# A gated cross-attention layer and a mixture of eight experts on one core: when the first rows, weights and output rows are moved, and which engine copies what

## The chip, the core and the metric

The kernel runs on one core of a Trainium2 chip. The core's engines take their instructions in program order, each from a queue of its own: TensorE (PE, with its weight loads shown apart as PEld), VectorE (DVE), ScalarE (ACT), GpSimd (POOL) and SyncE (SP). SP and POOL also start transfers (DMA); sixteen DMA engines move the bytes. The metric is the device time of one execution in microseconds (us). For the kernel before, three executions gave 212.71, 212.73 and 213.91 us, so a median of 212.73 us.

## The reference, cut to what matters

The input `x` is 4 batches of 256 rows of 256 numbers, `ctx` 4 x 256 x 128. First an attention layer adds to `x`, then a layer of experts adds to the sum:

```
query = ctx @ Wq.T + bq ;  key = ctx @ Wk.T + bk
attention = softmax(query @ key.T)
x = x + tanh(g0) * (layernorm(x) @ attention.T)          # per batch

xf = layernorm(x)
probs = softmax(gelu(xf @ rw1) @ rw2)
wgt, idx = top_k(probs, 2)                               # two of eight experts for each row
for e in range(8):
    Ye = gelu(xf @ w1[e] + b1[e]) @ w2[e] + b2[e]        # w1: 256 x 1024, w2: 1024 x 256
    Ce = gelu(b1[e]) @ w2[e] + b2[e]                     # what the expert gives for a row of zeros
    for k in range(2):
        mask = idx[:, k] == e ;  active = any(mask)
        out += active * wgt[:, k] * where(mask, Ye, Ce)
x = x + tanh(g1) * out
```

A row that did not choose expert e still receives `Ce`, weighted, if anybody chose it. So the output is x, plus for each row a constant part (a sum over experts of `Ce`), plus for its two chosen experts the difference `Ye - Ce`.

## The kernel before, in words

**Attention and router.** The 1024 rows are eight tiles of 128. Batches 0 to 2 (six tiles, "early") go through attention and the router first, in an order written by hand in a string (`order`, L446 to L453); batch 3 follows as steps that are woven into later work. Steps have names: `po` the attention product, `add` the sum into `acc` (the running x in SBUF), `sf`, `pf`, `xf` the second layer norm and its write to the table `rows` in DRAM (L367), `ow` the write of `acc` to the output in DRAM (L356). A step's name and a key (`ow:3`: batch 3; 2a and 2b are the two tiles of batch 2) make an entry.

**Slots.** The choices are sorted by expert into slots of 128 rows; a slot has one expert. Slots 0 to 4 hold early rows (NA = 5), slots 5 and up the rest; with this input 19 slots are used. Slots 0 to 15 are written out statically, 16 and up stand in conditional blocks. For each slot:
- `gather` (L764, on POOL) brings its 128 rows from `rows` by an index list (`take`), an indirect DMA;
- `fill` (L135, on SP) brings the expert's `w1` (1 MB); SP first reads the expert's number from the tile `who` (L893, `expert`). Slot 0's comes in two halves;
- `turn` transposes the rows on PE (L779) and copies them out of PSUM into `xs` (L781);
- `first_layer`: 8 chunks of four matmuls (L796), each closed by a gelu on ACT (L800); after four chunks DVE subtracts gelu(b1) (L803);
- `second_layer`, one slot behind: sixteen matmuls (L815) with `w2`, which lies in SBUF for all experts (`w2:5`, `w2:3` load it, L126); DVE scales the result by the rows' weights (L818) and POOL adds it into the output by an indirect DMA with add (L820).

Four PSUM banks take the first layer's results, two the second layer's, two (`bank_x`) the transposes and small products.

**Constants.** For every expert, DVE forms `gelu(b1) @ w2` down to 128 partial sums (`bias_path`, L842, eight instructions an expert, on the row `b2` loaded by `b2_`, L833 and L834) and adds it into `both` (L849, L851). One product with ones on PE (`sums1`, L875) adds the partitions, `sums2` (L878) copies it out of PSUM, `constant_row` (L884, L886) makes each tile's constant from it, and `add_constants` (L889, POOL) adds all to the output in one 1 MB DMA with add.

**Weaving.** Batch 3's router, the lists of the later slots, biases and constants are entries of two lists, `main` and `second`. `first_layer` and `second_layer` call `between` after every chunk, so sixteen times a slot; a call adds to a credit (0.45 us, less where DVE has work of the slot itself, at most 1.0 in all) and takes entries whose cost the credit still covers. A number in a list is a pause of so many calls. Entries issued in a call stand behind that chunk in every engine's queue:

```
credit = min(credit + us, 1.0)
...
if isinstance(queue[0], tuple) and queue[0][0] > 0 and credit < (-1.0 if name == "main" else 0.0):
    break
```

Where work between attention and slot 0 stands is written out (the block that begins with `do("cnt:0 tra:3 ...")`): index lists of the early slots, batch 3's attention, `gather:0`, `gather:1`, `fill:0` and `fill:1`, `turn(0)`.

Of the kernel before, what the change touches and what calls it, by code (L numbers as in the profile page):

```python
# [10 lines left out]
I32 = mybir.dt.int32  # L11
AF = mybir.ActivationFunctionType
# [7 lines left out]
def gated_xattn_moe_kernel(  # L20
# [417 lines left out]
    def w2_(n):  # L438
# [10 lines left out]
        attT:0 st:3 pw:3 xn:3 exp:1 po:0 attT:2 norm:1 po:2a add:0 pt:1 sf:0 po:2b attT:1 add:2a po:1 pf:0 add:2b sf:2a xf:0  # L449
        pf:2a add:1 trf:0 sf:2b xT:0 sf:1 pf:2b r:0 gel:0 xf:2b pf:1 xf:2a trf:2b lg:0 xT:2b trf:2a xf:1 w2:3  # L450
        r:2b xT:2a chosen:0 trf:1 gel:2b r:2a xT:1 lg:2b gel:2a chosen:2b r:1 lg:2a qk:3 gel:1 gb1 table:Exp q:3 k:3
        chosen:2a lg:1 chosen:1 ow:0 ow:2a ow:2b ow:1
    """  # L453
    MANUAL = {
        mybir.EngineType.PE, mybir.EngineType.Activation, mybir.EngineType.DVE, mybir.EngineType.Pool,
# [3 lines left out]
    def do(text):  # L459
        for step in text.split():  # L460
            kind, _, key = step.partition(":")
            steps[kind](key)
# [63 lines left out]
    nc.gpsimd.memset(runs1[:, 0:1], 0.0)  # L526
    nc.gpsimd.memset(runs2[:, 0:1], 0.0)

    hqs1 = last.tile([P, GA, P], BF16, name="hqs1")

    class Go:
# [240 lines left out]
    def turn(s, xs):  # L772

        if s >= NS:
            return
        xg = xgs.pop(s)
        ps = bank_x(f"xt_{s}")
        for c in range(DC):
            nc.tensor.transpose(ps[:, ts(c, P)], xg[:, ts(c, P)], ident)  # L779
        copy = nc.scalar.copy if s < NA else nc.vector.tensor_copy  # L780
        copy(xs, ps[:, 0:D].rearrange("p (c l) -> p c l", c=DC))  # L781
        xss[s] = xs

    def nothing(_):
# [24 lines left out]
    def second_layer(s, hT, between=nothing):  # L809
        go, j = of(s)  # L810
        e = nc.tensor.value_load(go.who[0:1, j : j + 1], min_val=0, max_val=E - 1)
        w2_sb = w2_all[:, bass.ds(e, 1)][:, 0]
        ps = bank_y(f"y_{s}")
        for i in range(IC):
            nc.tensor.matmul(ps[:, 0:D], lhsT=hT[:, i, :], rhs=w2_sb[:, i, :], start=(i == 0), stop=(i == IC - 1))  # L815
            between(0.45 - ((0.4 if s < NA else 0.8) if i == IC - 1 else 0.0))
        ys = slotp.tile([P, D], F32, tag="ys", bufs=4, name=f"ys_{s}")
        nc.vector.tensor_scalar(ys, ps[:, 0:D], go.share[:, j : j + 1], None, ALU.mult)  # L818
        last_row = EARLY * P if s < NA else T
        nc.gpsimd.indirect_dma_start(  # L820
            out=total[0:last_row, :], out_offset=bass.IndirectOffsetOnAxis(ap=go.give[:, j : j + 1], axis=0),
            in_=ys, in_offset=None, compute_op=ALU.add, bounds_check=last_row - 1, oob_is_err=False,
        )
# [56 lines left out]
    def constant_row(t, k):  # L880

        at = k * EARLY + t if t < EARLY else GA + k * LT + t - EARLY
        if k == 0:
            nc.vector.tensor_scalar(acc[:, t, :], sums[:, 0, :], wgt[:, at, :], None, ALU.mult)  # L884
        else:
            nc.vector.scalar_tensor_tensor(acc[:, t, :], sums[:, 1, :], wgt[:, at, :], acc[:, t, :], ALU.mult, ALU.add)  # L886

# [2 lines left out]

    def expert(s):
        go, j = of(s)
        return nc.sync.value_load(go.who[0:1, j : j + 1], min_val=0, max_val=E - 1)  # L893

    filled = 0

# [29 lines left out]
            inv_(i, g)  # L926

    with tc.manual_schedule(engines=MANUAL):
        do("cnt:0 tra:3 pc:0 scan en:3 xnT:3 over:0 runs:0 nmax:3 lead:0 exp:3 rank:0 pos:0 split:0 rden:3 put:0 norm:3 pt:3 attT:3")
        hqs_inv(0)  # L930
        do("past:0 who:0 fill:0 lists:0 gather:0 sel:0 soft:0 po:3 gather:1 fill:1")
        for i in range(2):
            bias_(0, i, 0, 1)
        do("wgt:0 add:3 table:Gelu ow:3")
        turn(0, transposed_rows(0))
        do("sf:3 pf:3 gather:4")
        for v in range(3):
            piece_(0, v)


        def each_(f, *args):
            return [(0.0, lambda a=a: f(*a)) for a in args]

        def w(cost, text):
            return cost, lambda: do(text)

        def f(cost, fn, *a):
            return cost, lambda: fn(*a)

        main = [  # L950
            3, w(.65, "xf:3"), 3, w(0, "trf:3"), 1, w(0, "xT:3"), 3, w(0, "r:3"), w(0, "gel:3"), 3, w(0, "lg:3"), 1,
            w(1.4, "chosen:3"), w(.2, "cnt:1"), 4, w(0, "pc:1"), w(.35, "scan"), w(.3, "soft:1"), w(.7, "over:1"),
            w(.3, "runs:1"), w(.5, "past:1"), w(.5, "who:1"), w(.45, "lead:1"), w(.4, "rank:1"), w(1.3, "pos:1"),
            w(.75, "split:1"), w(.6, "put:1"),
        ]
        for g in range(0, G, 4):
            main += [f(.16, hq_, 1, h) for h in range(g, g + 4)]
            main += [2] if g == 0 else []
            main += [f(0, inv_, 1, h) for h in range(g - 4, g)] if g else []
        main += [1] + [f(0, inv_, 1, h) for h in range(G - 4, G)] + [  # L960
            1, w(.35, "lists:1"), w(0, "gather:8 fill:7"), "lists", w(.25, "sel:1"),
        ]
        third = XS // 3
        main += [f(1.3, bias_, 1, i, 0, third) for i in range(2)] + ["biases 5", w(1.0, "wgt:1")]
        main += [f(.8, piece_, 1, v) for v in range(3)] + [2] + [f(0, inw_, 1, g) for g in range(G)] + [
            1, w(.25, "share:1"), "shares 1"] + [
            f(1.3, bias_, 1, i, lo, lo + third) for lo in (third, 2 * third) for i in range(2)] + ["biases 11"]
        main += [f(.2, act1_, 0), f(.2, act1_, 1), 2, f(0, act2_, 0), 1, f(.2, act3_, 0)]
        for e in range(E):
            main += [f(0, b2_, e)] if e else [f(0, b2_, 0)]  # L970
            main += [f(.47, bias_path, e, c) for c in range(IC)] + [f(.47, both_, e, k) for k in range(K)]
        main += [2, f(0, sums1_, 0), 2, f(.8, sums2_, 0)]
        main += [f(.47, constant_row, t, k) for t in range(NT) for k in range(K)] + [f(0, add_constants, 0)]
        second = [f(.6, bias_, 0, i, 1, 2) for i in range(2)] + ["biases 1"]
        second += [f(1.2, bias_, 0, i, 2, NA) for i in range(2)] + ["biases 2"]
        second = [5] + [f(0, inw_, 0, g) for g in range(GA)] + [2, w(.25, "share:0"), "shares 0"] + second
        queues = {"main": main, "second": second}
        credit, pause = 0.0, {"main": 0, "second": 0}
        reached = set()

        def one_item(name, forced=False):

            nonlocal credit
            item = queues[name].pop(0)
            if isinstance(item, str):
                reached.add(item)
            elif not isinstance(item, int):
                credit -= item[0]
                item[1]()
            elif not forced:  # L990
                pause[name] = item

        def between(us):
            nonlocal credit
            credit = min(credit + us, 1.0)
            for name, queue in queues.items():
                pause[name] = max(pause[name] - 1, 0)
                while queue and not pause[name]:
                    if isinstance(queue[0], tuple) and queue[0][0] > 0 and credit < (-1.0 if name == "main" else 0.0):
                        break  # L1000
                    one_item(name)

        def by_now(name, mark):
            while mark not in reached:
                one_item(name, forced=True)

        pending = None
        for s in range(FIX):
            if s > NA:
                gather_to(s + AHEAD)  # L1010
            if 0 < s < NA - 2:
                fill_to(s + 2)
            elif s > NA:
                fill_to(min(s + 2, FIX + 1))
            if s == NA - 1:
                by_now("main", "lists")
            if s > 0:
                turn(s + 1, transposed_rows(s + 1))
            if s in (1, 2):
                by_now("second", f"biases {s}")  # L1020
            if s in (NA, NA + third):
                by_now("main", f"biases {s}")
            hT = hidden(f"hT_{s}")
            first_layer(s, hT, between)
            if pending is not None:
                if pending[0] == 0:
                    by_now("second", "shares 0")
                if pending[0] == NA:
                    by_now("main", "shares 1")
                second_layer(*pending, between)  # L1030
            pending = (s, hT)
            if s == 0:
                turn(1, transposed_rows(1))
        assert gathered > FIX + AHEAD - 1 and filled == FIX + 2, (gathered, filled)
        while main:
            one_item("main", forced=True)
# [70 lines left out]
```

## Time and profile before

| | |
|---|---|
| median of three executions | 212.73 us |
| the profiled execution's own time | 212.38 us |
| its span, first to last instruction | 210.6 us |
| PE busy | 178.9 us, 85% |
| DVE busy | 142.2 us, 68% |
| ACT busy | 80.1 us, 38% |
| POOL busy | 72.7 us, 34% |
| moved by DMA | 38.76 MB, mean 184 GB/s |
| mean granted TensorE clock | 0.954 |

The profile is that of one execution. Its times count from the first instruction, so 1.8 us of the execution's time lie around the span. "Busy" is the time in which an engine executes; how long it waited, and what ended the wait, stands beside the groups of instructions. The clock is what the chip granted TensorE: 1.00 is full speed.

### The profile page before, as it was taken

Reading aid. Unit: us, or ns where it says so; the run is one execution under the profiler, and the core shown is the slowest. Engines: PE = TensorE matmul, PEld = TensorE weight load, DVE = VectorE, ACT = ScalarE, POOL = GpSimd, SP = SyncE. Lnnn points to the kernel's source line nnn. Section 1 sums busy time; section 2 is a strip of 40 time slices with the busy share of each in tenths; the row PEclk is TensorE's granted clock in tenths of the full one; section 3 lists DMA queues with packets and bytes.
Section 4 is the critical chain, followed back from the end, with each engine's and each line's share of the span. In section 5 each row is a group of like instructions: output and inputs, shape, how many; then the busy total and the mean of one; then the engine's idle time right before and its main releaser. Section 6 shows DMA issues by size and latency. Waiting matters only on the chain.

```text
span 210.6 us, 3835 instructions
## 1 busy us (share of the span) xinstructions
PE 178.9 (85%) x1198; PEld 159.7 (76%) x1198; DVE 142.2 (68%) x424; ACT 80.1 (38%) x210; POOL 72.7 (34%) x89
## 2 busy tenths in 40 slices
PE   2999762829799997999999999997499999999940
PEld 1866561619699897999999999995299989999830
DVE  1999888842478969978299999999589332242200
ACT  2582664404545143254245225423032451353100
POOL 5408200451008066041604422504531612545241
PEclk9999999676999999999999999999789999999995
DMA  6899999794793982225376678599502285332321
GB/s 180 243 329 351 335 293 341 244 335 177 251 344 70 366 299 76 28 25 199 78 291 181 192 226 251 209 373 372 160 7 48 47 111 91 50 54 31 55 30 20
DMA packets 23688, 38.76 MB, mean 184 GB/s; under 512 B 2440, under 2 KB 17808, under 8 KB 23664
## 3 DMA queue, kind: packets, MB, share of 16 engines
q1 hardware_dynamic: 18208, 32.16, 44.5%
q0 software_dynamic: 4880, 6.17, 16.8%
q8 instruction: 13, 0.21, 0.4%
q10 hardware_dynamic: 576, 0.13, 0.3%
q14 instruction: 11, 0.09, 0.1%
HBM read 33.21 MB, written 5.64 MB: 184 GB/s over the span
## 4 chain that ended last, share of the span: by engine, by line
DVE 20%; PE 14%; issue 12%; DMA 10%; POOL 2%; POOLq 0%; ACT 0%; DVEq 0%
DVE gsum L842 12%; PE h L796 7%; DMA out<-ys,give 6%; PE y L815 6%; DVE hT L803 4%; DMA out<-ys,take 3%; DVE both L851 2%; DVE ys L818 1%; PE cst L875 1%; POOL xg L764 1%; DVE xs L781 1%; POOL out L820 1%; DMA b_row<-in_b 1%; PE xt L779 0%; ACT hT L800 0%
## 5 line engine op out<-in xcount | busy, mean ns | idle before, releaser
L800 ACT ACTIVATE hT<-h,bsel 128x128 f32<-128x128 f32 x152 | 55.8, 367 | 82.4 <-PE h L796 65.3
L796 PE MATMUL h<-xs,w 128*128 128x128 f32 x608 | 75.1, 281 | 0.6 <-ACT xs L781 0.5
L796 PEld LDWEIGHTS h<-xs,w 128*128 128x128 f32 x608 | 72.1, 197 | 1.4 <-ACT xs L781 1.2
L815 PE MATMUL y<-w_all,hT 128*128 x304 | 70.2, 383 | 0.3 <-issue 0.3
L815 PEld LDWEIGHTS y<-w_all,hT 128*128 128x128 f32 x304 | 56.8, 192 | 8.4 <-issue 1.5
L820 POOL DMA_INDIRECT out<-ys,give x14 | 22.7, 1619 | 59.6 <-DVE ys L818 29.9
L803 DVE TENSOR_TENSOR hT<-hT,gbsel 128x512 f32<-128x512 f32 x38 | 26.2, 688 | 25.0 <-ACT hT L800 25.0
L764 POOL DMA_INDIRECT xg<-rows,take x23 | 24.3, 1058 | 22.7 <-DMA out<-acc 15.0
L842 DVE SCALAR_TENSOR_TENSOR gsum<-w_all,gb,gsum 128x256 f32<-128x256 f32 x56 | 27.0, 483 | 1.4
L818 DVE TENSOR_SCALAR ys<-y,share 128x256 f32<-128x256 f32 x19 | 9.1, 481 | 15.9 <-PE y L815 12.9
L820 POOL DMA_INDIRECT out<-ys,take x5 | 8.6, 1724 | 19.5 <-DVE ys L818 13.9
L779 PE MATMUL xt<-ident,xg 128*128 128x128 f32 x40 | 7.9, 284 | 5.2 <-issue 4.3
L779 PEld LDWEIGHTS xt<-ident,xg 128*128 128x128 f32 x40 | 5.5, 144 | 7.7 <-issue 4.7
L696 POOL TENSOR_TENSOR prob<-euler,prob 128x16 f32<-128x16 f32 x1 | 2.9, 2932 | 14.8 <-DVE capped L585 14.8
L339 PE MATMUL po<-attT,xnT 128*128 128x256 f32 x24 | 7.4, 464 | 0.0
L842 DVE SCALAR_TENSOR_TENSOR gsum<-w_all,gb,b_row 128x256 f32<-128x256 f32 x8 | 3.8, 481 | 4.7 <-DMA b_row<-in_b 4.7
L781 ACT COPY xs<-xt 128x256 f32<-128x256 f32 x5 | 1.8, 372 | 13.6 <-PE xt L779 13.6
L781 DVE COPY xs<-xt 128x256 f32<-128x256 f32 x15 | 6.2, 417 | 1.0 <-PE h L796 1.0
L299 POOL TENSOR_TENSOR rstd_a<-rstd_a,halves 128x2 f32<-128x2 f32 x4 | 3.0, 751 | 10.4 <-DVE rden L260 5.6
L851 DVE SCALAR_TENSOR_TENSOR both<-gsum,act,both 128x256 f32<-128x256 f32 x14 | 6.3, 482 | 0.2
L280 PE MATMUL pt<-ident,att 128*128 128x128 f32 x16 | 3.0, 293 | 4.0 <-ACT att L268 3.9
L339 PEld LDWEIGHTS po<-attT,xnT 128*128 128x128 f32 x24 | 5.4, 236 | 1.2 <-ACT attT L285 0.3
(201 smaller groups left out, 171.8 us busy)
## 6 DMA issues: line engine op xcount, KB each, us to landing
w<-in_w SPq DMA_DIRECT2D x18, 1024.0 KB, 5.9
w_all<-in_w SPq DMA_DIRECT2D x8, 1024.0 KB, 8.6
acc<-in_x SPq DMA_DIRECT2D x4, 256.0 KB
w<-in_w SPq DMA_DIRECT2D x2, 512.0 KB, 5.3
out<-acc POOLq DMA_DIRECT2D x1, 1024.0 KB, 9.4
rows<-xf SPq DMA_DIRECT2D x3, 256.0 KB
out<-acc SPq DMA_DIRECT2D x3, 256.0 KB
ctx_sb<-in_ctxT SPq DMA_DIRECT2D x3, 128.0 KB
```

The source lines that it names most:

```text
L339: nc.tensor.matmul(ps[:, ts(i, N)], lhsT=live["xnT", b][:, n, ts(t % LT, P)], rhs=live["attT", b][:, n, :], start=(n == 0), stop=(n == NN ...
L764: nc.gpsimd.indirect_dma_start(out=xg, out_offset=None, in_=rows[0 : EARLY * P if s < NA else T, :], in_offset=bass.IndirectOffsetOnAxis(a ...
L779: nc.tensor.transpose(ps[:, ts(c, P)], xg[:, ts(c, P)], ident)
L781: copy(xs, ps[:, 0:D].rearrange("p (c l) -> p c l", c=DC))
L796: nc.tensor.matmul(ps[:, 0:P], lhsT=w1_sb[:, c, ts(ch, P)], rhs=xs[:, c, :], start=(c == 0), stop=(c == DC - 1),)
L800: nc.scalar.activation(hT[:, ch, :], ps[:, 0:P], AF.Gelu, bias=bias[:, ch : ch + 1])
L803: nc.vector.tensor_tensor(hT[:, part, :], hT[:, part, :], gbias[:, part].rearrange("p (i o) -> p i o", o=1).to_broadcast([P, 4, P]), ALU.s ...
L815: nc.tensor.matmul(ps[:, 0:D], lhsT=hT[:, i, :], rhs=w2_sb[:, i, :], start=(i == 0), stop=(i == IC - 1))
L818: nc.vector.tensor_scalar(ys, ps[:, 0:D], go.share[:, j : j + 1], None, ALU.mult)
L820: nc.gpsimd.indirect_dma_start(out=total[0:last_row, :], out_offset=bass.IndirectOffsetOnAxis(ap=go.give[:, j : j + 1], axis=0), in_=ys, i ...
L842: nc.vector.scalar_tensor_tensor(gsums[e], w2_all[:, e, c, :], gb1[:, e, c : c + 1], b2_row[e % 2] if c == 0 else gsums[e], ALU.mult, ALU.add)
L851: nc.vector.scalar_tensor_tensor(both[:, k, :], gsums[e], a, both[:, k, :], ALU.mult, ALU.add)
```

## The change

Six edits:
1. The four `ow` entries leave the end of the hand-written order, and `ow:3` leaves its place behind `add:3`. All five now stand behind `turn(0)` and `fill:1`.
2. `past:0 who:0 fill:0` (slot experts known, w1 of slot 0 fetched) move from behind the index products to behind `runs:0`.
3. `fill:1` moves behind `turn(0)`. A new ACT instruction copies the five expert numbers into `who_later`; SP reads the experts of slots 1 to 4 from that copy.
4. The row copies of slots 5 and up (L781) go from DVE to ACT; slots 0 to 4 had theirs there already. The first of the two instructions of `constant_row` goes from DVE to ACT as well.
5. In `main`, the pause behind `piece_` grows from 2 to 5, that ahead of `sums1` from 2 to 10, that ahead of `sums2` from 2 to 3; the constant rows are spread with pauses of 2.
6. The second layer gives 0.4 more credit a slot from slot 5 on, and from the mark "shares 1" on `main` stops at a credit below 0 instead of below -1.

```diff
@@ order
-        chosen:2a lg:1 chosen:1 ow:0 ow:2a ow:2b ow:1
+        chosen:2a lg:1 chosen:1
@@
+    who_later = one([1, NA], "who_later", I32)
@@ turn
-        copy = nc.scalar.copy if s < NA else nc.vector.tensor_copy
-        copy(xs, ps[:, 0:D].rearrange("p (c l) -> p c l", c=DC))
+        nc.scalar.copy(xs, ps[:, 0:D].rearrange("p (c l) -> p c l", c=DC))
@@ second_layer
-            between(0.45 - ((0.4 if s < NA else 0.8) if i == IC - 1 else 0.0))
+            between(0.45 - (0.4 if i == IC - 1 else 0.0))
@@ constant_row
-            nc.vector.tensor_scalar(acc[:, t, :], sums[:, 0, :], wgt[:, at, :], None, ALU.mult)
+            nc.scalar.activation(acc[:, t, :], sums[:, 0, :], AF.Copy, scale=wgt[:, at, :])
@@ expert
-        return nc.sync.value_load(go.who[0:1, j : j + 1], min_val=0, max_val=E - 1)
+        src = who_later if 0 < s < NA else go.who
+        return nc.sync.value_load(src[0:1, j : j + 1], min_val=0, max_val=E - 1)
@@ manual schedule
-        do("cnt:0 tra:3 pc:0 scan en:3 xnT:3 over:0 runs:0 nmax:3 lead:0 exp:3 rank:0 pos:0 split:0 rden:3 put:0 norm:3 pt:3 attT:3")
+        do("cnt:0 tra:3 pc:0 scan en:3 xnT:3 over:0 runs:0 past:0 who:0 fill:0 nmax:3 lead:0 exp:3 rank:0 pos:0 split:0 rden:3 put:0 norm:3 pt:3 attT:3")
         hqs_inv(0)
-        do("past:0 who:0 fill:0 lists:0 gather:0 sel:0 soft:0 po:3 gather:1 fill:1")
+        do("lists:0 gather:0 sel:0 soft:0 po:3 gather:1")
         for i in range(2):
             bias_(0, i, 0, 1)
-        do("wgt:0 add:3 table:Gelu ow:3")
+        do("wgt:0 add:3 table:Gelu")
         turn(0, transposed_rows(0))
-        do("sf:3 pf:3 gather:4")
+
+        nc.scalar.copy(who_later, go1.who[:, 0:NA])
+        do("fill:1 ow:0 ow:2a ow:2b ow:1 ow:3 sf:3 pf:3 gather:4")
@@ main
-        main += [f(.8, piece_, 1, v) for v in range(3)] + [2] + [f(0, inw_, 1, g) for g in range(G)] + [
+        main += [f(.8, piece_, 1, v) for v in range(3)] + [5] + [f(0, inw_, 1, g) for g in range(G)] + [
@@
-        main += [2, f(0, sums1_, 0), 2, f(.8, sums2_, 0)]
-        main += [f(.47, constant_row, t, k) for t in range(NT) for k in range(K)] + [f(0, add_constants, 0)]
+        main += [10, f(0, sums1_, 0), 3, f(.8, sums2_, 0)]
+        for t in range(NT):
+            main += [f(0, constant_row, t, 0), 2, f(.47, constant_row, t, 1)]
+        main += [f(0, add_constants, 0)]
@@ between
-                    if isinstance(queue[0], tuple) and queue[0][0] > 0 and credit < (-1.0 if name == "main" else 0.0):
+                    if isinstance(queue[0], tuple) and queue[0][0] > 0 and credit < (0.0 if name == "second" or "shares 1" in reached else -1.0):
```

## The prediction, made before the change was run

> **What bounds the kernel now.** I read the list of waits of PE first, because PE is busy 85% of the span and is the engine to which most of the chain leads. Columns: us in total, times, longest.
>
> ```profile
> PE cst L875 <- DVE both L851: 4.6, 1, 4.6
> PE xt L779 <- issue: 4.3, 1, 4.3
> PE qk L223 <- DMA wq_sb<-in_wqT: 3.9, 1, 3.9
> PE pt L280 <- ACT att L268: 3.9, 1, 3.9
> ...
> PE inw L727 <- DVE putw L719: 1.2, 1, 1.2
> ```
>
> After attention PE stands idle in three places only: 4.3 us before slot 0's transposes, 1.2 before `inw` of the later slots, 4.6 before the constants' product `cst`. Between them it is full (41.87 of 42 us from 104 to 146), so time won at one of them reaches the end, if the end follows PE. It does: the last two sums `ys` (L818) end 3.5 us apart behind PE's last products, and the scatter before last (199.77) starts 0.3 us after its `ys`.
>
> Then the timeline around the first place, for what "issue" hides:
>
> ```profile
> 39.49 1.22 POOL L764 DMA_INDIRECT xg<-rows,take  x1 [14.95 <-DMA out<-acc]
> 39.52 2.18 SPq L135 DMA_DIRECT2D w<-in_w  x3
> ...
> 45.85 0.66 PE L779 MATMUL xt<-ident,xg 128*128 128x128 f32 x2 [4.30 <-issue]
> 46.55 0.37 ACT L781 COPY xs<-xt 128x256 f32<-128x256 f32 x1 [5.66 <-PE xt L779]
> ```
>
> `gather:0` goes out at 39.49 and PE starts at 45.85. The DMA view of that moment, and of a gather at 77.69 (issue, KB, us to landing), gives the reason:
>
> ```profile
> xg<-rows,take POOLq DMA_INDIRECT x1, 6.3
> ```
> ```profile
> xg<-rows,take POOLq DMA_INDIRECT x1, 2.8
> ```
>
> The first lands at 45.8, just before PE starts; the second needs 2.8. Ahead of the first go the output rows of four `ow` (768 KB, issued from 29.69 on, through near 39.5), beside it slot 0's weights, which start only at 39.52 and, with slot 1's, keep the DMA share at 0.9 to 1.1 from 41 to 49.
>
> Last the granted clock, in windows (start:end, length, PE busy, instructions, clock, DMA share, GB/s):
>
> ```profile
> 30.87:34.28 3.41, 1.65 (x11) 1.00 0.97 299
> 34.28:37.70 3.42, 1.29 (x22) 1.00 1.09 362
> 37.70:41.11 3.41, 3.41 (x15) 0.50 0.61 207
> 41.11:44.52 3.41, 0.45 (x2) 1.00 1.02 332
> 44.52:47.94 3.42, 1.62 (x6) 0.50 0.97 331
> 47.94:51.35 3.41, 3.41 (x18) 0.50 0.56 205
> ...
> 146.92:150.34 3.42, 0.00 (x0) 1.00 0.62 232
> 150.34:153.75 3.41, 3.25 (x6) 0.50 0.37 75
> ```
>
> Each idle stretch is paid twice: a window with 0.00, 0.45 or 1.29 us of PE work is followed by half speed, one with 1.65 was not.
>
> **Part by part.** The sum is made against the profiled execution's own 212.38 us; the median is 0.35 more, added at the end.
>
> *Output rows and w1 of slot 0 (edits 1, 2).* The five `ow` leave the queue. The last `w2` was issued by 29.7, so SP is free for `fill:0` when `who` is ready, about 33, six us sooner. DVE pays: `past` and `who` cost 0.55 (37.89 to 38.44); ahead of `nmax` it was idle 0.40, so the path through softmax and `po` is late by 0.2. `take` becomes ready 0.2 late, `gather:0` goes out at 39.7. `w2` and the `ow` finished near 39.5; with 1 MB of w1 in the place of 0.77 MB they finish near 40 to 41. So the gather meets an almost free queue: rows for such gathers are 2.8, 3.0 and 3.5 us (77.69, 78.97, 76.25); bounds are 6.3 again, or landing before `po` ends at 41.75. I take 3.2, the middle of the three: landing at 42.9. From the transposes to slot 0's first product were 1.13 us, so it starts at 44.0 instead of 46.98: **3.0** won (0 to 4.1).
>
> *The half speed behind it.* Slot 0 ran at half clock from 46.98 to 51.35: 2.2 us lost. With the new start the window 41.11 to 44.52 holds 0.64 us of `po`, 0.5 of transposes, 0.5 of slot 0: 1.6, between the 1.29 that dropped the clock and the 1.65 that kept it. Won are 2.2, or, if it drops for one window, 2.2 - 1.7 = 0.5. I take the middle, **1.3**. [...]
>
> *`fill:1` behind ACT's copy (edit 3).* A new wait: `who_later` comes after slot 0's row copy on ACT (44.2), SP needs 1.0 us from `who` to issue (38.52 to 39.52), so w1 of slot 1 goes out at 45.2; with the median landing of 5.9 us it is there by 51.1. Behind it on SP wait the `ow`, batch 3's `rows` and `fill:2`, none needed before 60. Slot 1's first product was 8.57 us after slot 0's; with 1.3 of clock won it is due at 51.3. So about nothing is lost, but the first two terms can't give much more than 4.4: I subtract **0.2**.
>
> *`inw` (edit 5).* `putw` ends at 83.85, PE arrives at 82.7. Three more calls of 0.45 (16 calls a slot, slots 7.24 apart) put PE at 84.1, and DVE is 0.33 earlier without a row copy: **1.1** won.
>
> *The constants' product (edits 4 to 6).* Counting pauses and credits through the lists: `sums1` stood behind the fourth chunk of slot 11's second layer (the trace has `cst` between y x8 and y x8) and now stands behind its eighth, 4 x 0.43 = 1.7 us later for PE. The last `both` is issued four calls earlier than before.
>
> ```profile
> 145.27 0.59 PE L815 MATMUL y<-w_all,hT 128*128 x2
> 150.50 2.05 PE L875 MATMUL cst<-both,ones 128*128 128x512 f32 x2 [4.63 <-DVE both L851]
> 152.34 2.59 PE L815 MATMUL y<-w_all,hT 128*128 x8
> ```
>
> From 105.39, when expert 1's `b_row` arrives, to 150.36 DVE is busy 43.5 of 45.0 us: it is the bound of this stretch, not its place in the order. Its chain loses six row copies (x 0.33, 2.0 us), one correction `hT` that now follows the last `both` (0.60), and starts 1.2 earlier: `ys` of slot 4 then has four instead of seven terms of expert 0 ahead of it, and the scatter, two gathers and memset on POOL before `b_row` hang on that `ys`. So DVE ends at 150.4 - 3.8 = 146.6, PE comes at 145.87 + 1.7 = 147.6: the wait of 4.6 goes. What is late next is PE itself. With the idle window goes the half clock of 150.34: `cst` 2.05 becomes 1.0, half a `y` 2.4 becomes 1.7 (half of a full one, 3.46): 1.7 more. **6.3** together; at the lower bound DVE gains nothing and the term is 1.7.
>
> *Copies on ACT.* A copy is 0.37 us, as on slots 0 to 4. Cover: PE may run four banks (1.8 us) ahead of the gelus, and ACT rests 3.8 us between first layers. At nothing; uncovered it would be 14 x 0.37 = 5.2. The eight constant rows (0.47 each by L268) put three into one first layer, 1.4 us on top of 3.5 + 0.37 against PE's 3.6: cost **0.3** at most once.
>
> *The tail.* `add_constants` keeps its place (one call later). In before it holds the scatters back from 167.55 to 177.72, and they have caught up at 192.52, 0.3 us after `ys`; the same shape, earlier.
>
> Sum: 3.0 + 1.3 - 0.2 + 1.1 + 6.3 - 0.3 = 11.2. 212.4 - 11.2 = 201.2, and with the median's 0.35 **201.5 us**.
>
> **Rivals.**
> *The gather stays slow.* w1 of slot 0 now moves at the time when `ow` moved; the landing is again 6.3 and the first two terms vanish: 212.7 - 7.1 = 205.6. For it: the gathers at 39.49 and 41.01, beside weights, took 6.3 and 6.6. Against: by 41 those weights are through. [...]
> *DVE is as late as before.* If its lag comes from elsewhere than its work, PE waits 2.9 at `cst` instead of 4.6; the term is 1.7 instead of 6.3: 206.1. Against: gaps of 0.02 us between its instructions on the chain.
> *The order is not the limit* (the edits don't do what they say): both of these at once, little left but `inw`: 211.6.
> *Slower: ACT becomes the bound of the first layer.* If the gelus of a slot could start only after transposes (0.38), a wait of 0.3 and the copy (0.37), and PE did not run ahead, a first layer would take 3.49 + 1.05 = 4.5 instead of 3.6: 0.97 for each of 14 slots, 13.6 us, 215.1. It decides from 11.2 / 14 = 0.8 us a slot on. Against: in slots 1 to 4, which had this order, PE waited for `xs` 0.5 us in all.
>
> **How the numbers follow.** Forecast 0.62, gather 0.14, DVE 0.12, order 0.06, ACT 0.06. A measurement of this kernel can tell about 1% (2.1 us) from no change. Faster by over 1%: the first three, 0.88; within 1%: 0.06; slower 0.06. The forecast's own range: 200 (gather 4.1, clock 2.2, of which the weights of slot 1 take back 0.9 more) to 204 (gather 1.4, clock 0.5). Below, the half clock at 37.70 may go too (1.7): low 198.3. High 206.4 takes in the gather and DVE rivals. That leaves out the last two, 0.12.
>
> **What would show it.** Right: `xt` starts before 43.5 and its "issue" wait is under 1.5; no wait of PE at `cst` over 1 us and no half-clock window near it; `inw` gone from the list; the scatters at the end as close to `ys` as now. Wrong: a gather above 5 us, a wait of slot 1 for its weights, PE idle before L796 in each slot, or DVE gaps between its `gsum` terms, which would mean that SP's `b_row` loads pace it.

## The result

The changed kernel takes **203.14 us** (median of six executions, 202.11 to 203.56). The kernel before, run beside it, took 213.32 (212.46 to 216.13). The ratio is 0.9517 [0.9467, 0.9566]: faster by 10.2 us, where 11.2 (201.5 us) had been forecast. The profiled executions differ by 9.5: 212.38 and 202.87, with spans of 210.6 and 201.1.

The list of waits of PE after the change (us in total, times, longest):

```profile
PE pt L280 <- ACT att L268: 4.0, 1, 4.0
PE qk L223 <- DMA wq_sb<-in_wqT: 3.4, 1, 3.4
PE tra L324 <- DVE hot L414: 1.5, 1, 1.5
PE xt L780 <- ACT xT L374: 0.9, 1, 0.9
PE r L381 <- ACT xT L374: 0.8, 2, 0.7
PE trf_2b L324 <- DVE xf_2b L304: 0.8, 1, 0.8
PE xt L780 <- DMA xg<-rows,take: 0.5, 1, 0.5
PE xt L780 <- PE po L339: 0.5, 1, 0.5
PE h L796 <- ACT xs L781: 0.5, 1, 0.5
PE qk L223 <- DMA ctx_sb<-in_ctxT: 0.4, 1, 0.4
```

The three waits that the prediction went by are gone or small: `cst` and `inw` are no longer in the list, and the 4.3 us of "issue" before slot 0 have become 0.5 behind `po`. There is a new line, though: 0.5 for a gather. The timeline shows that it is the third one, with slot 2's rows, which PE transposes ahead of slot 1's first layer. These are the rows of the timeline after the change around the first slots (start us, us, engine, line, operation, out<-in; in brackets the idle time before it and what ended it):

```profile
35.54 11.11 SPq L135 DMA_DIRECT2D w<-in_w  x3
...
41.20 1.22 POOL L765 DMA_INDIRECT xg<-rows,take  x1 [15.01 <-ACT prob L695]
...
44.34 0.66 PE L780 MATMUL xt<-ident,xg 128*128 128x128 f32 x2 [0.51 <-PE po L339]
...
45.47 4.34 PE L796 MATMUL h<-xs,w 128*128 128x128 f32 x24 [0.46 <-ACT xs L781]
...
46.69 2.93 SPq L356 DMA_DIRECT2D out<-acc  x5
...
47.04 1.02 POOL L765 DMA_INDIRECT xg<-rows,take  x1 [0.19 <-issue]
...
53.55 0.41 PE L780 MATMUL xt<-ident,xg 128*128 128x128 f32 x2 [0.54 <-DMA xg<-rows,take]
```

`gather:0` goes out at 41.20 and PE starts on its rows at 44.34, 3.1 us later; before, these were 39.49 and 45.85, 6.4 apart. But the five `ow`, which now go out from 46.69 on, and the weights of slot 1 ahead of them meet the third gather (47.04), and that one now takes 6.4 us (5.5 in the kernel before). It stands so in the chain that ended last, with its start and length:

```profile
47.04 6.37 DMA xg<-rows,take
```

The clock in windows (start:end, length, then busy time and instructions of PE, PEld, DVE, ACT and POOL, granted clock, DMA share, GB/s):

```profile
34.77:38.18 3.41, 0.00 (x0) 0.00 (x0) 3.20 (x19) 1.51 (x6) 0.00 (x0) 1.00 1.07 362
38.18:41.59 3.41, 3.33 (x32) 2.83 (x33) 2.98 (x18) 1.68 (x5) 0.39 (x1) 0.50 1.03 362
41.59:45.00 3.41, 2.90 (x8) 1.54 (x6) 2.29 (x10) 1.06 (x2) 1.82 (x2) 0.50 0.33 105
45.00:48.42 3.42, 2.96 (x15) 2.95 (x15) 1.95 (x13) 1.19 (x4) 1.80 (x3) 0.50 0.22 22
48.42:51.83 3.41, 3.22 (x36) 2.92 (x35) 1.34 (x3) 1.93 (x6) 2.14 (x2) 1.00 0.93 318
```

The DMA share tells why the first gather became quick: at 41.59 the weights of slot 0 are through and the share falls from 1.03 to 0.33. The clock did not get better: three windows at half speed, from 38.18 to 48.42, cover `po` (3.78 us) and most of slot 0's first layer.

Around the constants' product, after the change:

```profile
142.79 0.48 DVE L851 SCALAR_TENSOR_TENSOR both<-gsum,act,both 128x256 f32<-128x256 f32 x1
144.55 1.02 PE L875 MATMUL cst<-both,ones 128*128 128x512 f32 x2
```

The last `both` ends at 143.27, `cst` starts 1.3 us later without a wait, and it takes 1.02 instead of 2.05.

Where the time went follows from the start of each slot's first product `h` in the two traces. Up to the scan `runs` no edit touches what it waits for:

| | before | after | won so far |
|---|---|---|---|
| scan `runs` (DVE) starts | 31.93 | 33.60 | -1.67 |
| slot 0 | 46.98 | 45.47 | 1.51 |
| slot 1 | 55.55 | 53.83 | 1.72 |
| slot 2 | 64.47 | 62.72 | 1.75 |
| slot 4 to slot 5 | 9.08 | 7.94 | 1.14 in this step |
| slot 12 to slot 13 | 14.59 | 8.11 | 6.48 in this step |
| slots 13 to 16 | 22.29 | 22.11 | 0.18 in this step |
| last slot to the end of the span | 18.82 | 18.86 | -0.04 in this step |

The later part gave what was expected of it, and a little more. The start gave 1.75 instead of 4.1. 1.67 of that was lost before the first edit acts. The same two rows in both traces show it; first the kernel before, then the changed one:

```profile
7.23 0.59 PE L223 MATMUL qk<-ctx_sb,wq_sb 128*128 128x256 f32 x2
```
```profile
7.93 1.06 PE L223 MATMUL qk<-ctx_sb,wq_sb 128*128 128x256 f32 x2
```

The same pair of products takes 0.59 us in one execution and 1.06 in the other. In the first PE came to full speed near 7.0 us, in the second near 10.9. This is read from the lengths of the products; the rows of the granted clock show 1.00 in both stretches. In the second PE had also waited 0.4 us for `ctx_sb`.

### The profile page after: what moved, and what is told of

It is laid out like the page before. It is cut to its first block, busy times and chain, and to the rows that moved or that the text cites. A ratio compares the mean times of both kernels' runs of the same rounds, so it can differ in the third digit from the quotient of the medians.

```text
span 201.1 us, 3845 instructions
## 1 busy us (share of the span) xinstructions
PE 178.9 (89%) x1198; PEld 159.3 (79%) x1198; DVE 134.7 (67%) x401; ACT 88.1 (44%) x234; POOL 73.1 (36%) x89
## 4 chain that ended last, share of the span: by engine, by line
PE 65%; DMA 14%; DVE 11%; issue 6%; POOL 1%; ACT 1%; SPq 0%; POOLq 0%; ACTq 0%; DVEq 0%
PE h L796 27%; PE y L815 26%; DMA out<-ys,give 8%; DMA xg<-rows,take 3%; PE qk L223 2%; DMA ctx_sb<-in_ctxT 2%; PE po L339 2%; PE xt L780 2%; DVE acc L353 1%; DVE nmax L246 1%; DVE att L272 1%; DVE st_f L292 1%; PE r L381 1%; PE inv L655 1%; POOL out L820 1%
## 5 line engine op out<-in xcount | busy, mean ns | idle before, releaser
L796 PE MATMUL h<-xs,w 128*128 128x128 f32 x608 | 74.1, 279 | 0.5 <-ACT xs L781 0.5
L815 PE MATMUL y<-w_all,hT 128*128 x304 | 69.5, 381 | 0.1
L815 PEld LDWEIGHTS y<-w_all,hT 128*128 128x128 f32 x304 | 56.1, 190 | 7.2 <-issue 0.3
L781 ACT COPY xs<-xt 128x256 f32<-128x256 f32 x20 | 7.5, 372 | 61.7 <-PE xt L780 61.7
L765 POOL DMA_INDIRECT xg<-rows,take x23 | 25.0, 1085 | 22.7 <-ACT prob L695 15.0
L223 PE MATMUL qk<-ctx_sb,wq_sb 128*128 128x256 f32 x6 | 3.5, 686 | 3.8 <-DMA wq_sb<-in_wqT 3.4
L280 PEld LDWEIGHTS pt<-ident,att 128*128 128x128 f32 x16 | 1.9, 156 | 5.5 <-ACT att L268 4.4
```

Source lines behind the costliest of these rows:

```text
L223: nc.tensor.matmul(dst, lhsT=w, rhs=ctx3 if b == "3" else ctx_sb[:, int(b), :], start=True, stop=True)
L765: nc.gpsimd.indirect_dma_start(out=xg, out_offset=None, in_=rows[0 : EARLY * P if s < NA else T, :], in_offset=bass.IndirectOffsetOnAxis(a ...
L781: nc.scalar.copy(xs, ps[:, 0:D].rearrange("p (c l) -> p c l", c=DC))
L796: nc.tensor.matmul(ps[:, 0:P], lhsT=w1_sb[:, c, ts(ch, P)], rhs=xs[:, c, :], start=(c == 0), stop=(c == DC - 1),)
```

## The experiments

All ratios are to the kernel before, run beside each. "Since `runs`" is counted from the start of the scan `runs` of the same trace, so that a late start of the clock drops out. For comparison: the kernel before has slot 0 at 15.05 since `runs` and slot 2 at 32.54; the changed one has 11.87 and 29.12.

**1. The two halves.** The first kernel has edits 1 to 3 alone, the second edits 4 to 6 alone.

```diff
# e4_start_only: the changed kernel with edits 4 to 6 undone
-        main += [10, f(0, sums1_, 0), 3, f(.8, sums2_, 0)]
+        main += [2, f(0, sums1_, 0), 2, f(.8, sums2_, 0)]
...
-        nc.scalar.copy(xs, ps[:, 0:D].rearrange("p (c l) -> p c l", c=DC))
+        copy = nc.scalar.copy if s < NA else nc.vector.tensor_copy
+        copy(xs, ps[:, 0:D].rearrange("p (c l) -> p c l", c=DC))
...
# e5_weave_only: the kernel before with edits 4 to 6
-        main += [2, f(0, sums1_, 0), 2, f(.8, sums2_, 0)]
+        main += [10, f(0, sums1_, 0), 3, f(.8, sums2_, 0)]
...
```

> Edits 1 to 3 alone (output rows, slot 0's weights, slot 1's weights), with the weaving and copies of the kernel before. Theory (the stretch that DVE bounds hangs on PE, so that what is won at the start is carried to the end): 3.5 to 4 us below the kernel before, about 209.5, with the waits of 1.2 at `inw` and 4.6 at `cst` as before. Rival (DVE's stretch has a clock of its own and the start's gain is lost in it): 212 to 213, with a longer wait at `cst`.

> Edits 4 to 6 alone (copies on ACT, pauses, credits), with the start of the kernel before. Theory: 7.5 us below the kernel before, about 205.8: the waits at `inw` (1.2) and `cst` (4.6) and the half-clock window behind `cst` (1.7) are gone, the 4.3 us before slot 0 stay. Rival (DVE is as late as before): a wait of some 3 us at `cst`, 208 to 210.

Edits 4 to 6 alone: 205.62 us, 0.9632 [0.9611, 0.9653], as expected. Neither `cst` nor `inw` is left in PE's waits, and the wait of 3.3 before slot 0 stays. Edits 1 to 3 alone: 211.56 us, 0.9904 [0.9876, 0.9931], 2 us slower than expected. Its waits of PE:

```profile
PE cst L876 <- DVE both L852: 4.6, 1, 4.6
...
PE xt L780 <- ACT xT L374: 2.2, 1, 2.2
...
PE xt L780 <- DMA xg<-rows,take: 1.0, 1, 1.0
PE inw L728 <- DVE putw L720: 1.0, 1, 1.0
```

Slot 0 began at 43.99, 11.95 since `runs`: the full 3.1 us are won there. But two waits stand behind it, 2.2 for batch 3's transposed rows `xT`, which ACT copies behind slot 0's last gelu, and 1.0 for the third gather. The window that follows them runs at half clock (slot 1's first 12 products take 2.77 us, 1.58 in the changed kernel), and slot 2 begins at 63.15, 31.11 since `runs`. So of 3.1 only 1.4 arrive. PE came earlier to a place whose inputs had not become earlier by as much. What held ACT there is not shown: slot 0's seventh gelu starts at 49.29, 1.95 us after the one before it had ended, though its product was done by 47.8. The two halves' gains, 3.7% and 1.0%, add up to 4.6%, against 4.8% for the whole change.

**2. What holds the first gather: the output rows ahead of it, or the weights beside it?** The prediction named both. The first kernel puts the `ow` back to the front, the second leaves them behind and puts the weights of slot 0 back beside the gather, the third gives the weights of slot 1 their old place.

```diff
# e1_ow_back
-        chosen:2a lg:1 chosen:1
+        chosen:2a lg:1 chosen:1 ow:0 ow:2a ow:2b ow:1
-        do("fill:1 ow:0 ow:2a ow:2b ow:1 ow:3 sf:3 pf:3 gather:4")
+        do("fill:1 ow:3 sf:3 pf:3 gather:4")
# e6_fill0_late
-        do("... over:0 runs:0 past:0 who:0 fill:0 nmax:3 ...")
+        do("... over:0 runs:0 nmax:3 ...")
-        do("lists:0 gather:0 sel:0 soft:0 po:3 gather:1")
+        do("past:0 who:0 fill:0 lists:0 gather:0 sel:0 soft:0 po:3 gather:1")
# e7_fill1_early: the number of slot 1's expert is read from `who`
-        do("lists:0 gather:0 sel:0 soft:0 po:3 gather:1")
+        do("lists:0 gather:0 sel:0 soft:0 po:3 gather:1 fill:1")
-        do("fill:1 ow:0 ow:2a ow:2b ow:1 ow:3 sf:3 pf:3 gather:4")
+        do("ow:0 ow:2a ow:2b ow:1 ow:3 sf:3 pf:3 gather:4")
-        src = who_later if 0 < s < NA else go.who
+        src = who_later if 1 < s < NA else go.who
```

> The changed kernel with the output rows (the five `ow`) back in their old places, ahead of slot 0's weights; the weights of slots 0 and 1 stay where the change put them. Theory (what stands ahead in SP's queue holds POOL's gather up): the gather of slot 0, about 3.1 us in the changed kernel, takes 4.5 to 6 us to land, and slot 0's first product comes 1.5 to 3 us later after the gather goes out; 204.6 to 206, against 203.1 of the changed kernel. [...]

> The changed kernel with `past`, `who` and the first weights back in their old place behind the index products (edit 2 undone; output rows and slot 1's weights stay late). Theory now (the gather of slot 0 is held up by weights that move beside it, not by rows ahead of it in SP's queue): slot 0's weights go out within 0.3 us of the gather, the gather takes 4.5 to 6 us instead of 3.1, slot 0's first product comes 1.5 to 2.5 us later. By slot 2 a part of that is lost anyway to the wait for gather 2; 204 to 205 against 203.1. Rival (the output rows were what mattered): gather 3.1, 203.1 or a little less, since DVE is relieved ahead of `nmax`.

> The changed kernel with slot 1's weights right behind slot 0's (edit 3 undone). Theory: now 2 MB of weights move from 36 to about 44, the gathers of slots 0 and 1 meet the second of them and take 5 to 6.5 us instead of 3; slot 0 starts 2 to 3 us later. Gather 2 and slot 1's weights are then free of each other, which gives back the 0.5 us of slot 1; 204 to 205.5. Rival (the wait on ACT's copy costs as much as it saves): 203.1 or below.

With the `ow` back, 204.04 us, 0.9562 [0.9496, 0.9627]; the interval overlaps with that of the whole change. The timeline of this kernel:

```profile
39.68 1.22 POOL L765 DMA_INDIRECT xg<-rows,take  x1 [15.23 <-DMA out<-acc]
...
43.37 0.41 PE L780 MATMUL xt<-ident,xg 128*128 128x128 f32 x2 [1.07 <-issue]
```

From issue to PE's start are 3.7 us. The output rows went out ahead of slot 0's weights here, and the weights are what still moves: the DMA share is 1.00 and 0.81 in the two microseconds from 40 to 42. Slot 0 stands at 12.39 since `runs`, 0.5 later than with the change. With `fill:0` late, 205.64 us, 0.9625 [0.9544, 0.9706]:

```profile
41.59 1.22 POOL L765 DMA_INDIRECT xg<-rows,take  x1 [14.95 <-ACT prob L695]
41.63 8.04 SPq L135 DMA_DIRECT2D w<-in_w  x3
...
47.37 0.66 PE L780 MATMUL xt<-ident,xg 128*128 128x128 f32 x2 [3.31 <-issue]
```

No output rows ahead, but slot 0's weights issued at the same moment: 5.8 us. With `fill:1` early, 205.2 us, 0.9631 [0.9574, 0.9688]:

```profile
39.69 1.22 POOL L765 DMA_INDIRECT xg<-rows,take  x1 [14.99 <-ACT prob L695]
...
45.86 0.41 PE L780 MATMUL xt<-ident,xg 128*128 128x128 f32 x2 [3.54 <-issue]
```

Slot 0's weights early, slot 1's and the output rows issued directly behind them, still moving when the gather goes out: 6.2 us.

The DMA share of the kernel before says what the output rows did there (start:end, length, clock, DMA share, GB/s):

```profile
39.00:40.00 1.00, 0.50 0.48 170
40.00:41.00 1.00, 0.50 0.16 43
41.00:42.00 1.00, 0.94 0.90 246
```

They were all but through when the first gather went out at 39.49; what came next was slot 0's weights. The theory that the output rows held the gather of the kernel before falls. In steps of 0.1 us the DMA view also tells when POOL's queue moves the first packet of a gather:

| gather | issued | first packet after |
|---|---|---|
| changed kernel, first | 41.20 | 1.9 |
| `ow` back, first | 39.68 | 1.9 |
| kernel before, first | 39.49 | 4.4 |
| `fill:0` late, first | 41.59 | 4.4 |
| `fill:1` early, first | 39.69 | 4.4 |
| changed kernel, third | 47.04 | 5.0 |

Where the gather is long, it has been held ahead of its first packet, while SP's queue moves: 1.02 MB between 39.49 and 43.9 in the kernel before, 1.21 MB between 47.04 and 52.0 for the third gather of the changed one. In each of these cases SP had sent out 1 MB or more that had not moved yet: slot 0's weights 0.03 and 0.04 us behind the gather (kernel before, `fill:0` late), slot 1's weights and four output writes, the last of them begun 1.7 us ahead of it (`fill:1` early), slot 1's weights 0.8 us ahead (the third gather). With the `ow` back the last transfer had gone out at 36.45 and was nearly through. So in these four cases transfers that SP sent out shortly ahead of the gather or together with it held it, by 2.5 to 3.1 us ahead of its first packet (4.4 to 5.0 instead of 1.9), output rows perhaps as well as weights. How they did that is not shown.

Edits 2 and 3 are both needed for the 3 us: without one of them slot 0 stands at 14.44 and 14.64 since `runs`. In the times only the second of these is clear of the whole change's interval. Edit 1 gives 0.5 of it in this profile, and nothing that the intervals can tell.

**3. The constants' product: its place, or DVE's relief?** The first kernel undoes the longer pauses ahead of `sums1` and `sums2` alone, the second puts the row copies of slots 5 and up and the first half of each constant row back on DVE.

```diff
# e2_cst_early
-        main += [10, f(0, sums1_, 0), 3, f(.8, sums2_, 0)]
+        main += [2, f(0, sums1_, 0), 2, f(.8, sums2_, 0)]
# e3_copies_dve
-        nc.scalar.copy(xs, ps[:, 0:D].rearrange("p (c l) -> p c l", c=DC))
+        copy = nc.scalar.copy if s < NA else nc.vector.tensor_copy
+        copy(xs, ps[:, 0:D].rearrange("p (c l) -> p c l", c=DC))
...
-            nc.scalar.activation(acc[:, t, :], sums[:, 0, :], AF.Copy, scale=wgt[:, at, :])
+            nc.vector.tensor_scalar(acc[:, t, :], sums[:, 0, :], wgt[:, at, :], None, ALU.mult)
```

> The changed kernel with the two pauses around `sums1` back at 2 and 2; copies on ACT and the new credits stay. PE then comes to the constants' product eight calls, some 3.5 us, earlier than in the changed kernel, where the last `both` ended 1.3 us before PE came. Theory (DVE's lighter load did part, the later place the rest): PE waits 2 to 2.5 us at `cst`, in all 205 to 206, and up to 1.7 more if the idle stretch costs a half-clock window. Rival A (the later place did it all): the wait is 4.6 again and the half clock comes, 209. Rival B (DVE's relief did it all): no wait, 203.1.

> The changed kernel with the row copies of slots 5 and up and the first instruction of the constant rows back on DVE; pauses and credits stay. Theory (the work on DVE sets when `both` is done): DVE ends 2.0 to 2.5 us later between expert 1's start and the last `both`, where the changed kernel had 1.3 us to spare: a wait of 0.7 to 1.2 at `cst`, 203.8 to 204.3. Rival (the later place alone was enough): no wait, 203.1.

With the old pauses, 207.82 us, 0.974 [0.9692, 0.9787]; with the copies on DVE, 204.7 us, 0.9583 [0.9514, 0.9651]. The wait of PE in each:

```profile
PE cst L875 <- DVE both L851: 2.7, 1, 2.7
```
```profile
PE cst L876 <- DVE both L852: 0.8, 1, 0.8
```

The place is worth more. PE comes to `cst` 78.5 us behind slot 2's start instead of 81.8. That is 3.3 earlier, and eight calls of 0.43 are 3.4. DVE is ready only at 81.1, and the half-clock window from 143.7 to 147.1 follows the wait. By the ratios this costs 2.2%, 4.7 us. Without the relief DVE's last `both` ends 83.0 behind slot 2's start instead of 80.6. It is 2.4 us later, 1.3 were to spare, and the wait is 0.8. By the ratios that costs 0.7%, 1.4 us, with an interval that overlaps the whole change's.

**4. The gathers of slots 2 and 3 ahead of the moved transfers.** `gather:1` sends the second gather, of slot 1's rows; `gather:3` sends the third and fourth as well, before POOL takes up batch 3's normalization.

```diff
# e8_gathers_first
-        do("lists:0 gather:0 sel:0 soft:0 po:3 gather:1")
+        do("lists:0 gather:0 sel:0 soft:0 po:3 gather:3")
```

> The changed kernel with the gathers of slots 2 and 3 directly behind that of slot 1 on POOL, ahead of `pf:3`. They go out from 44 on, before slot 1's weights (46.3) and the output rows; gather 2 then takes 3 to 4.5 us instead of 6.4, and PE's wait of 0.5 us for it ahead of slot 1 goes. If that gather is what holds slot 1: 202.4 to 202.8. If the batch-3 chain (`xT`, 0.9 us) or slot 1's weights hold it as well: 203.1.

200.86 us (200.43 to 202.0), **0.9435 [0.9378, 0.9491]**, against the whole change's 203.14; all four executions lie below all six of the changed kernel, while the two intervals still overlap. Its timeline:

```profile
42.92 0.95 POOL L765 DMA_INDIRECT xg<-rows,take  x1 [0.30 <-issue]
...
45.37 3.09 SPq L356 DMA_DIRECT2D out<-acc  x5
...
51.24 1.58 PE L796 MATMUL h<-xs,w 128*128 128x128 f32 x12 [0.62 <-DMA w<-in_w]
```

The third gather leaves at 42.92, 2.5 us ahead of the `ow` instead of just behind them. Slot 1 begins 7.09 behind slot 0 (8.36 in the changed kernel) and slot 2 at 27.92 since `runs`, 1.2 earlier. Slot 1 now waits for its weights, 0.6, which are in the chain that ended last: that is what is late next. A part of the step from slot 0 to slot 1 is the clock: in this execution slot 0's 24 products ran at full speed (2.94, against 4.34). Experiment 6 comes back to that.

**5. Products that keep the clock up.** The half speed at `po` and slot 0 follows a window in which PE does nothing (34.77 to 38.18 in the changed kernel, 0.00 us of work). These kernels add products of ones that nobody reads: 12 ahead of `qk`, 8 ahead of `tra:3`, 20 ahead of `pt:3`. The first adds them to the change, the second to experiment 4.

```diff
# e9_warm (e10_both: the same and gather:3)
...
+    def warm_up(n):
+        ps = late_bank["warm"]("warm") if "warm" in late_bank else bank("warm")
+        for _ in range(int(n)):
+            nc.tensor.matmul(ps[:, 0:P], lhsT=ones, rhs=ones, start=True, stop=True)
-        w2:5 table:Tanh g ident qk:0
+        w2:5 table:Tanh g ident warm:12 qk:0
-        do("cnt:0 tra:3 pc:0 ...
+        do("cnt:0 warm:8 tra:3 pc:0 ...
-        ... norm:3 pt:3 attT:3")
+        ... norm:3 warm:20 pt:3 attT:3")
```

> The changed kernel with products of ones on PE that nobody reads (128x128, 12 ahead of the first `qk`, 8 ahead of `tra:3`, 20 ahead of `pt:3`), in stretches in which PE waits. They add work and no result. Theory (the idle stretches from 28 to 38 put PE at half clock for 10 us, from 38.2 to 48.4 in the changed kernel, in which `po` and part of slot 0 run): no half-clock window between 12 and 190, `po` and slot 0 3 us sooner, 199.5 to 201. Rival (slot 1's start is set by gather 2 and slot 1's weights anyway): `po` is sooner, but the gather follows DVE and slot 1 waits more; 202 to 203.

> The products of ones and the gathers of slots 2 and 3 directly behind that of slot 1, in the changed kernel. Theory: the two add up, since the gathers took away what held slot 1: 197.5 to 199, with slot 1's weights (0.6 us of waiting without the products) as the next wait. Rival (slot 1's weights take it all): 200.9, as with the gathers alone.

206.03 us, 0.9655 [0.9604, 0.9706], and 204.11, 0.9577 [0.9529, 0.9625]: each about 3 us slower than the same kernel without them. From the timeline of the second, which records each product of ones twice:

```profile
31.91 2.05 PE L441 MATMUL warm<-ones 128*128 128x128 f32 x16 [1.42 <-ACT k L233]
...
35.26 4.63 PE L441 MATMUL warm<-ones 128*128 128x128 f32 x40
39.72 0.60 PE L280 MATMUL pt<-ident,att 128*128 128x128 f32 x4
...
41.14 1.97 PE L339 MATMUL po<-attT,xnT 128*128 128x256 f32 x8
...
45.53 0.41 PE L785 MATMUL xt<-ident,xg 128*128 128x128 f32 x2 [2.42 <-issue]
```

`po` takes 1.97 instead of 3.78, so the clock does stay up there. It drops later: in the second kernel slot 0's 24 products take 4.57, in the first slot 1's first 12 take 2.63 instead of 1.58. And `runs` starts at 35.58 and 34.80, later than in any kernel without them (31.85 to 34.05), since the eight products ahead of `tra:3` hold it up by their own length, 3.3 us in the first kernel and 1.9 in the second. Behind `po` PE waits 2.4 us for the first gather. The 1.8 us won at `po` had been time in which the gather was still under way.

**6. The weight softmax out of the gather's way, and a few products at one place.** The row of `gather:0` names ACT's `prob` as its releaser. The first kernel takes experiment 4 and moves `soft:0` behind the first biases; the second adds ten products of ones ahead of `pt:3` alone.

```diff
# e11_soft_later
-        do("lists:0 gather:0 sel:0 soft:0 po:3 gather:3")
+        do("lists:0 gather:0 sel:0 po:3 gather:3")
-        do("wgt:0 add:3 table:Gelu")
+        do("soft:0 wgt:0 add:3 table:Gelu")
# e12_soft_warm: the same and
-        ... norm:3 pt:3 attT:3")
+        ... norm:3 warm:10 pt:3 attT:3")
```

> The changed kernel with the gathers of slots 2 and 3 behind that of slot 1 (as in the run of the gathers before) and with `soft:0` (DVE, then an exp on ACT) moved behind the first biases. In before and in the changed kernel gather 0 goes out 0.9 us after `take` is written and 0.06 to 0.12 us after that exp has ended. If it waits for the exp in some way, it now goes out at another distance from `take`; if sooner, slot 0 comes up to 0.6 us sooner (PE waits 0.6 for the gather), 200.3. If the 0.9 us are GpSimd's own, the distance stays 0.9 and the time 200.9.

> As the run before, with ten products of ones that nobody reads between `en:3` and `pt:3` alone (2.3 us of PE where it waits about 4). Theory (in the run with forty of them in three places they stood in the way of `tra:3`, `pc` and `pt:3`; in the gap alone they only keep the clock up): `pt`, the index products and `po` run at full clock, gather 0 goes out 0.5 to 0.8 us sooner and slot 0 with it; 199.5 to 200.3. Rival (they still delay `pt`, or slot 1's weights hold slot 1): 200.9 or above.

201.22 us (200.34 to 203.34), 0.9433 [0.9394, 0.9473], and 201.86, 0.947 [0.9441, 0.9498]. Neither differs from experiment 4 by more than the intervals. The first contains experiment 4 and so repeats its gain over the change. The timeline of the first:

```profile
40.29 0.17 DVE L663 TENSOR_SCALAR take<-inv 128x5 int32<-128x5 f32 x1 [0.31 <-PE inv L655]
41.34 1.23 POOL L765 DMA_INDIRECT xg<-rows,take  x1 [15.94 <-DMA w<-in_w]
...
42.16 0.24 ACT L695 ACTIVATE prob<-prob 128x48 f32<-128x48 f32 x1 [2.01 <-DVE prob L692]
```

`prob` now comes after the gather, and the gather still goes out 0.88 us behind the end of `take`, as in the changed kernel (40.30 to 41.20, 0.90). The releaser named in the row was a coincidence in time. In the second kernel `po` ended at 40.93, and PE then waited:

```profile
PE xt L785 <- issue: 2.3, 1, 2.3
...
PE h L801 <- DMA w<-in_w: 0.9, 1, 0.9
```

So slot 0 hangs on the chain index list, 0.9 us, gather, 3 us, and not on `po` or its clock; and slot 1 on its weights. In all kernels with a quick first gather except the one with `ow` back PE starts 3.0 to 3.2 us after its issue. The wait of 0.5 that the list of the changed kernel puts down to `po` is therefore one for the gather as well.

What the gathers of experiment 4 win depends on the clock in slot 0:

| | slot 0's 24 products | from slot 0 to slot 2 |
|---|---|---|
| changed kernel | 4.34 | 17.25 |
| experiment 6, first kernel (gathers first) | 4.60 | 17.19 |
| edits 1 to 3 alone; `ow` back | 2.94; 2.94 | 19.16; 18.48 |
| experiment 4; experiment 6, second kernel (gathers first) | 2.94; 2.94 | 15.99; 16.27 |

Where slot 0 ran at half speed, sending the gathers first won nothing in the profile, and that execution, at 203.34, was the slowest of its six. Where slot 0 ran at full speed, it won 2.2 to 3.2 us. These are single profiles; the medians contain both kinds in shares that are not known.

## Why the prediction was right, and where it was not

**The constants' product (6.3):** 6.48 from slot 12 to slot 13. DVE was forecast ready 1.0 us ahead of PE and was 1.3 ahead. The half speed behind the wait went with it, as forecast. In experiment 3's profiles the wait comes back without either half of the step, 2.7 us without the place and 0.8 without the relief; the times tell only the first from the whole change.

**`inw` (1.1):** 1.14 from slot 4 to slot 5; the wait is gone from the list.

**Copies on ACT (-0.3 at most):** nothing to be seen. From slot 5 to slot 12, with row copies alone, it is 50.97 in both traces; from slot 13 to slot 16, with the constant rows as well, 22.11 instead of 22.29. **The tail:** 18.86 against 18.82, as said.

**The first gather (3.0):** right in size: 3.18 since `runs`, and 3.10 in experiment 1, while 0.6 and 0.4 are left of it without edit 2 or edit 3. One sign named for it, `xt` before 43.5, did not come (44.34); without the 1.67 lost ahead of `runs` it would have been 42.67. Its reason was half wrong. The prediction put the output rows ahead of the gather beside the weights as its cause. By its own figure they were through near 39.5, when the gather went out, and the DMA share in experiment 2 says the same. In a long gather 4.4 us or more go by ahead of its first packet while SP's queue moves, and only then do both move side by side: in the kernel before 29 packets of POOL's queue and 47 of SP's from 43.9 to 44.4. What makes the gather wait so long is not shown. The first rival did not come about, since by 41.6 the weights of slot 0 were through.

**`fill:1` behind ACT's copy (-0.2):** this step failed. It counted what waits behind `fill:1` in SP's queue and found nothing needed before 60. It did not look at what runs beside it: POOL's third gather, issued at 47.04 behind the normalization of batch 3, whose rows PE transposes ahead of slot 1. A gather above 5 us was one of the prediction's signs of being wrong; it came, at another gather than the one it was meant for. Edit 3 takes the transfer away from the first gather and lays it on the third, which then takes 6.4 us. In the changed kernel PE waits only 0.5 for it, because slot 0 ran slowly. Where slot 0 ran at full speed, in experiment 1's first kernel, PE waited 2.2 and 1.0 there and lost the next window's clock as well. Experiment 4 removes the wait for the gather, and that for `xT` is back at 0.9. The latter stood in the list of the kernel before, and the prediction's "three places only" put it at nothing:

```profile
PE xt L779 <- ACT xT L374: 0.9, 1, 0.9
```

**The half speed behind it (1.3):** slot 0's first layer went from 5.02 to 4.34, 0.7 won; at full speed these 24 products took 2.94. That 0.7 lies between the two ends of the term is chance, since other windows were slow than those it was made from. The three windows from 38.18 to 48.42 were not foreseen: the prediction laid the new work into the windows of the old execution, and reckoned with one slow window at most. In the rows above, windows at half speed with 3.33 and 2.90 us of PE work were followed by another slow one, and one with 2.96 by full speed. In the other executions half speed lay at 31.4 to 51.9 (edits 4 to 6 alone) or 31.9 to 42.2 (`ow` back). And the term was not one to be added: what a better clock wins at slot 0 is lost again at slot 1, as long as the third gather, and `xT` ahead of it, come no earlier (the table in experiment 6).

**The sum.** Profiled against profiled 11.2 was forecast and 9.5 came. Before slot 2 it is 1.75 instead of 4.1: 1.67 of the difference lies ahead of `runs`, and 0.7 is the failed step with the clock term. From slot 2 on it is 7.75 instead of 7.1. That the 1.67 is the phase of the clock at the start is read from single profiles (7.0 against 10.9 us until full speed), not tested; over all kernels with the same code ahead of `runs` it began between 31.85 and 34.05. How much of the scatter between medians of similar kernels comes from it stays open.

## What to carry to other kernels

When a large transfer is moved away from a small one that something waits for, look at which small transfer it runs beside next; sending the small gathers first was worth about 2 us here (200.86 and 201.22 against 203.14). A wait for another engine can be removed by moving the waiting product back as far as its own result allows, which gave more here than relieving the engine did (2.2% against 0.7% in experiment 3). Time won at one place counts only up to the next thing that has not become earlier by as much: name it before adding the terms.

## What the runs showed of the hardware that was not expected

- A gather of 128 rows took 3.0 to 3.2 us from issue to use where the DMA share fell soon after its issue (1.03 to 0.33 in the changed kernel), and 5.8 to 6.5 in the four cases of experiment 2 in which it was held. The difference lies ahead of its first packet: 1.9 us from issue in the quick ones, 4.4 to 5.0 in the others.
- The first gather goes out 0.9 us after its index list is ready, also where ACT's `prob` comes later (0.88 in experiment 6).
- Full speed came first near 7.0 us from the start of the span in the kernel before and near 10.9 in the changed one, with the same code up to there, as read from the lengths of the products; `runs` began up to 2.2 us apart (31.85 with `ow` back, 34.05 with `fill:0` late).
- Half speed outlasted windows of 3.41 us in which PE worked for 3.33 and 2.90 us (38.18 to 45.00 in the changed kernel).
- Products that nobody reads did keep the clock up at `po` (1.97 instead of 3.78), not in the slots behind it (slot 0's 24 products 4.57 in one kernel, slot 1's first 12 2.63 in the other, against 2.94 and 1.58 at full speed), and still made the kernel slower by about 3 us: eight of them held up needed work by 1.9 to 3.3 us, and the gain at `po` fell into a wait for a gather.
